# A graph layer and a routed expert layer on one core: slot heads one slot ahead, and results added by scatters into DRAM

## The chip, the cores and the metric

The kernel runs on one core of one Trainium2 chip. The metric is the device time of one execution in microseconds (us), the median of several. The other cores of the chip do nothing here.

## What is computed

There are 2048 nodes with 256 float32 features each. A first layer normalises every row, gathers neighbours along 67,584 weighted edges and adds the sums (and a per-node value) to the input. A second layer normalises again and sends every row to the best 2 of 8 experts. Cut to what matters:

```python
x = x + segment_sum(edge_weight[:, None] * layernorm(x)[dst], src) + node_vec1   # "x1" below
t = layernorm(x)
probs = softmax(t @ Wr + br)                      # 2048 x 8
top_p, top_idx = top_k(probs, 2)
weights = top_p / top_p.sum(-1, keepdims=True)
xn = layernorm(t)
# for each of the two experts e of a row:
h = gelu((xn * ln_g[e] + ln_b[e]) @ W1[e] + b1[e])          # 256 -> 1024
y = h @ W2[e] + b2[e]                                        # 1024 -> 256
out = x + weights[0] * y[top_idx[0]] + weights[1] * y[top_idx[1]]
```

So every output row is x1 plus two expert results, each multiplied by its weight.

## The kernel before

The first part (up to about 319 us of the profile) builds x1 in an SBUF tile `acc` of 128 partitions x 16 blocks x 256 and is the same in both kernels. Then a routing part ranks every (row, expert) pair and makes a dispatch list: the rows of each expert lie together, and each expert's rows are padded up to whole *slots* of 256 rows. There are at most 23 slots; 16 always exist, the others stand under conditions. Rows travel to their places in a DRAM buffer `xe_d` by 32 indirect DMAs (scatters) of 128 rows from the GpSimd queue. A row takes along its two expert numbers, its two weights and its token number (columns 256 to 260).

```python
y_d = dram.tile([2 * N + NS * TS, D], F32, name="y_d")       # N = 2048, NS = 23, TS = 256, D = 256
# ... routing ...
sent = []
for b in range(NB):                                          # NB = 16
    for i in range(2):
        st = nc.gpsimd.indirect_dma_start(out=xe_d[:, :],
            out_offset=bass.IndirectOffsetOnAxis(ap=rows_i[:, i, b:b + 1], axis=0),
            in_=xrow[:, b, :], in_offset=None)
        sent.append(st.ins.name)
# ... the bias b2, weighted, is added to acc by 16 small matmuls and adds (L556, L557) ...
```

Then the slots run one after the other. There are three sets of buffers; slot s + 2 is loaded while slot s computes. All loads go out on the SyncE queue, in this order per slot: the slot's rows, W1 of its expert (1 MB), a small tile of columns `ec` (bias and norm scales), W2 (1 MB).

```python
def load_slot(s):
    xs, w1, w2, ec = sets[s % len(sets)]
    ld = nc.sync.dma_start(xs, xe_v[s])                      # L592, waits for all 32 scatters of `sent`
    nc.sync.dma_start(w1, W1[e]...)                          # L595
    nc.sync.dma_start(ec, cols_d[e]...)                      # L596
    nc.sync.dma_start(w2, W2[e]...)                          # L597

def run_slot(s):
    # head: turn the rows (4 transposes of 128x128), scale them, find weight and target of each row
    for t in range(TT):                                      # TT = 2
        for k in range(KD):                                  # KD = 2
            nc.tensor.transpose(pt[:, k, ...], xs[:, t, ...], ident)       # L604, tile px
    for k in range(KD):
        nc.vector.tensor_scalar(xeT[:, k, :], pt[:, k, :], ec[...], ec[...], ...)   # L608
    # mine, wr, wt, any, to, to_i: eight small VectorE operations on 128x2 or 128x4 (L613 to L627);
    # to_i = 2 * token + (0 or 1), or a spare row for padding
    # body
    for c in range(KH):                                      # KH = 8
        ... ph = W1 chunk x xeT (2 matmuls, L633); hT[:, c] = gelu(ph) on ScalarE (L635)
    for t in range(TT):
        ... py = hT x W2 (8 matmuls, L639)
        nc.vector.tensor_scalar(ys, py, wt[:, t:t + 1], None, op0=OP.mult)          # L642
        nc.gpsimd.indirect_dma_start(out=y_d[:, :], out_offset=...to_i[:, t:t + 1]...,
                                     in_=ys, in_offset=None)                        # L643
```

Each float32 matmul of the code is recorded as two on the PE. At the end the two results of every row, which lie side by side in `y_d`, are read back (4 DMAs of 1 MB), added to `acc` by eight VectorE additions, and written out (4 DMAs of 512 KB):

```python
for q in range(NB // 4):
    ld = (nc.sync, nc.scalar)[q % 2].dma_start(yy, y_v[:, s, :])       # L672, waits for every scatter of results
    for r in range(2):
        nc.vector.tensor_add(acc[:, s, :], acc[:, s, :], yy[:, :, r * D:(r + 1) * D])   # L676
    (nc.sync, nc.scalar)[q % 2].dma_start(out_v[:, s, :], acc[:, s, :])  # L677
```

Of the kernel before, what the change touches and what calls it, by code (L numbers as in the profile page):

```python
# [20 lines left out]
P = 128  # L21
# [4 lines left out]
def kernel(  # L26
# [60 lines left out]
    for q in range(4):  # L87
# [32 lines left out]
    keep = consts.tile([P, NE, NB], F32, name="keep")  # L120
    nc.vector.memset(keep, 1.0)
    nc.vector.memset(keep[:, :, 0:1], 0.0)
    tok2 = consts.tile([P, NB], F32, name="tok2")
    nc.gpsimd.iota(tok2, pattern=[[2 * P, NB]], base=0, channel_multiplier=2,
                   allow_small_or_imprecise_dtypes=True)
    spare_r = consts.tile([P, NS, TT], F32, name="spare_r")
    nc.gpsimd.iota(spare_r, pattern=[[TS, NS], [P, TT]], base=2 * N, channel_multiplier=1,
                   allow_small_or_imprecise_dtypes=True)
    slot_e = consts.tile([P, NS], F32, name="slot_e")
    slot_i = consts.tile([1, NS + 1], I32, name="slot_i")  # L130
    xe_d = dram.tile([NS * TS, RW], F32, name="xe_d")
    y_d = dram.tile([2 * N + NS * TS, D], F32, name="y_d")
    cols_d = dram.tile([NE, P, KH + 2 * KD], F32, name="cols_d")
    none = consts.tile([P, RW], F32, name="none")
    nc.vector.memset(none, 0.0)
# [282 lines left out]

    with tc.tile_pool(name="route", bufs=1) as route, tc.tile_pool(
        name="xtT", bufs=3
    ) as xtTp, tc.tile_pool(name="ps_tr", bufs=3, space=PSUM) as ps_tr, tc.tile_pool(
# [1 line left out]
    ) as ps_lg, tc.tile_pool(name="ps_b2", bufs=2, space=PSUM) as ps_b2:  # L426
        xt = route.tile([P, NB, D], F32, name="xt")
        xrow = route.tile([P, NB, RW], F32, name="xrow")
        nc.vector.tensor_copy(xrow[:, :, D + 4:D + 5], tok2[:, :, None])
        nc.vector.memset(xrow[:, :, D + 5:], 0.0)  # L430
        mv, rs = stats(acc, "mva")
        for b in range(NB):
            normed(xt[:, b, :], acc[:, b, :], mv, rs, b)
# [120 lines left out]
        for b in range(NB):  # L554
            pb = ps_b2.tile([P, D], F32, name="pb")
            nc.tensor.matmul(pb, wgtT[:, b, :], b2_sb, start=True, stop=True)  # L556
            nc.vector.tensor_add(acc[:, b, :], acc[:, b, :], pb)  # L557


    got = []  # L560
    with tc.tile_pool(name="wpool", bufs=1) as wpool, tc.tile_pool(
        name="slot", bufs=2
    ) as slotp, tc.tile_pool(
        name="ps_x", bufs=1, space=PSUM
    ) as ps_x, tc.tile_pool(name="ps_h", bufs=4, space=PSUM) as ps_h, tc.tile_pool(
        name="ps_y", bufs=2, space=PSUM
    ) as ps_y:
        _, offs = nc.values_load_multi_w_load_instructions(
            slot_i[0:1, :NS], engines=[mybir.EngineType.SP], min_val=0, max_val=NE - 1,
            skip_runtime_bounds_check_because="a count of at most NE - 1 ends",  # L570
        )
        _, (n_slots,) = nc.values_load_multi_w_load_instructions(
            slot_i[0:1, NS:NS + 1], min_val=N * 2 // TS, max_val=NS,
            skip_runtime_bounds_check_because="the sum of the experts' slots",
        )
        xe_v = xe_d.rearrange("(s t p) c -> s p t c", t=TT, p=P)

        sets = []
        for i in range(AHEAD + 1):
            sets.append((  # L580
                wpool.tile([P, TT, RW], F32, name=f"xs{i}"),
                wpool.tile([P, KD, H], F32, name=f"w1_{i}"),
                wpool.tile([P, KH, D], F32, name=f"w2_{i}"),
                wpool.tile([P, KH + 2 * KD], F32, name=f"ec{i}"),
            ))

        def load_slot(s):
            if s >= NS:
                return
            e = ds(offs[s], 1)  # L590
            xs, w1, w2, ec = sets[s % len(sets)]
            ld = nc.sync.dma_start(xs, xe_v[s])  # L592
            for name in sent:
                tc.add_manual_dep(ld.ins, name, WAITS, reason="reads what it wrote")
            nc.sync.dma_start(w1, W1[e].rearrange("o (k p) h -> p (o k) h", p=P))  # L595
            nc.sync.dma_start(ec, cols_d[e].rearrange("o p c -> p (o c)"))  # L596
            nc.sync.dma_start(w2, W2[e].rearrange("o (c p) d -> p (o c) d", p=P))  # L597

        def run_slot(s):
            xs, w1, w2, ec = sets[s % len(sets)]  # L600
            pt = ps_x.tile([P, KD, TS], F32, name="px")
            for t in range(TT):
                for k in range(KD):
                    nc.tensor.transpose(pt[:, k, t * P:(t + 1) * P],  # L604
                                        xs[:, t, k * P:(k + 1) * P], ident)
            xeT = slotp.tile([P, KD, TS], F32, name="xeT")
            for k in range(KD):
                nc.vector.tensor_scalar(xeT[:, k, :], pt[:, k, :], ec[:, KH + k:KH + k + 1],  # L608
                                        ec[:, KH + KD + k:KH + KD + k + 1],
                                        op0=OP.mult, op1=OP.add)  # L610

            mine = slotp.tile([P, TT, 2], F32, name="mine")
            nc.vector.tensor_scalar(mine, xs[:, :, D:D + 2], slot_e[:, s:s + 1], None,  # L613
                                    op0=OP.is_equal)
            wr = slotp.tile([P, TT, 2], F32, name="wr")
            nc.vector.tensor_mul(wr, mine, xs[:, :, D + 2:D + 4])
            wt = slotp.tile([P, TT], F32, name="wt")
            nc.vector.tensor_reduce(wt, wr, AX.X, OP.add)
            spare = spare_r[:, s, :]
            any_ = slotp.tile([P, TT], F32, name="any")  # L620
            nc.vector.tensor_reduce(any_, mine, AX.X, OP.add)
            to = slotp.tile([P, TT], F32, name="to")
            nc.vector.tensor_sub(to, xs[:, :, D + 4], spare)
            nc.vector.tensor_mul(to, to, any_)
            nc.vector.tensor_add(to, to, mine[:, :, 1])
            to_i = slotp.tile([P, TT], I32, name="to_i")
            nc.vector.tensor_add(to_i, to, spare)  # L627

            hT = slotp.tile([P, KH, TS], F32, name="hT")
            for c in range(KH):  # L630
                ph = ps_h.tile([P, TS], F32, name="ph")
                for k in range(KD):
                    nc.tensor.matmul(ph, w1[:, k, c * P:(c + 1) * P], xeT[:, k, :],  # L633
                                     start=(k == 0), stop=(k == KD - 1))
                nc.scalar.activation(hT[:, c, :], ph, AF.Gelu, bias=ec[:, c:c + 1], scale=1.0)  # L635
            for t in range(TT):
                py = ps_y.tile([P, D], F32, name="py")
                for c in range(KH):
                    nc.tensor.matmul(py, hT[:, c, t * P:(t + 1) * P], w2[:, c, :],  # L639
                                     start=(c == 0), stop=(c == KH - 1))  # L640
                ys = slotp.tile([P, D], F32, name="ys")
                nc.vector.tensor_scalar(ys, py, wt[:, t:t + 1], None, op0=OP.mult)  # L642
                st = nc.gpsimd.indirect_dma_start(  # L643
                    out=y_d[:, :],
                    out_offset=bass.IndirectOffsetOnAxis(ap=to_i[:, t:t + 1], axis=0),
                    in_=ys,
                    in_offset=None,
                )
                tc.declare_no_dep(st.ins, group="got", reason="rows are unique")
                tc.add_to_no_dep_group("got", st.ins)  # L650
                got.append(st.ins.name)

        SURE = N * 2 // TS
        for s in range(AHEAD):
            load_slot(s)
        for s in range(SURE):
            load_slot(s + AHEAD)
            run_slot(s)
        with ExitStack() as nest:
            for s in range(SURE, NS):  # L660
                nest.enter_context(tc.If(n_slots > s))
                load_slot(s + AHEAD)
                run_slot(s)


    with tc.tile_pool(name="fin", bufs=4) as fin:
        out_v = out.rearrange("(b p) d -> p b d", p=P)
        y_v = y_d[:2 * N, :].rearrange("(b p r) d -> p b (r d)", p=P, r=2)
        for q in range(NB // 4):
            s = slice(4 * q, 4 * q + 4)  # L670
            yy = fin.tile([P, 4, 2 * D], F32, name="yy")
            ld = (nc.sync, nc.scalar)[q % 2].dma_start(yy, y_v[:, s, :])  # L672
            for name in got:
                tc.add_manual_dep(ld.ins, name, WAITS, reason="reads what it wrote")
            for r in range(2):
                nc.vector.tensor_add(acc[:, s, :], acc[:, s, :], yy[:, :, r * D:(r + 1) * D])  # L676
            (nc.sync, nc.scalar)[q % 2].dma_start(out_v[:, s, :], acc[:, s, :])  # L677


# [22 lines left out]
```

## Time and profile before

| | |
|---|---|
| time, median of 3 runs | 718.31 us (717.87 to 719.97) |
| span of the profiled execution | 719.2 us, mean granted TensorE clock 0.910 |
| PE busy, weight loads (PEld) busy | 538.0 us (75%), 468.5 us (65%) |
| VectorE, ScalarE, GpSimd busy | 314.8, 161.2, 99.6 us |
| DMA | 75.85 MB, mean 105 GB/s |

The execution falls into three parts: the graph layer up to 319 us, routing and dispatch from there to 414 us, and 18 slots (16 certain ones and two of the conditional ones) followed by the final sums. In the profile's groups, the two columns behind the bar are the busy time of a group and the mean duration of one instruction in ns, and then the idle time of the engine before them with the name of what ended it. PE is the matmul, PEld the weight load beside it, DVE VectorE, ACT ScalarE, POOL GpSimd; an engine with a q (SPq) is its queue of DMA issues. A DMA issue shows only when it was handed over; when it landed is read from who waited for it.

### The profile page before, as it was taken

Reading aid. Unit: us, or ns where it says so; the run is one execution under the profiler, and the core shown is the slowest. Engines: PE = TensorE matmul, PEld = TensorE weight load, DVE = VectorE, ACT = ScalarE, POOL = GpSimd, SP = SyncE. Lnnn points to the kernel's source line nnn. Section 1 sums busy time; section 2 is a strip of 40 time slices with the busy share of each in tenths; the row PEclk is TensorE's granted clock in tenths of the full one; section 3 lists DMA queues with packets and bytes.
Section 4 is the critical chain, followed back from the end, with each engine's and each line's share of the span. In section 5 each row is a group of like instructions: output and inputs, shape, how many; then the busy total and the mean of one; then the engine's idle time right before and its main releaser. Section 6 shows DMA issues by size and latency. Waiting matters only on the chain.

```text
span 719.2 us, 12356 instructions
## 1 busy us (share of the span) xinstructions
PE 538.0 (75%) x5244; PEld 468.5 (65%) x5244; DVE 314.8 (44%) x768; ACT 161.2 (22%) x309; POOL 99.6 (14%) x112
## 2 busy tenths in 40 slices
PE   0002789998998999968480099999999999999930
PEld 0001687897897889757340078888878888787730
DVE  6636999858947863137650022121121211211105
ACT  1001443135216205102100022222223222222200
POOL 1771000000000000000067301111111111111110
PEclk9999989999999999995555589999999999999985
DMA  8920000000000000000022495546456455565428
GB/s 258 349 53 19 2 3 3 1 3 3 2 1 3 3 1 3 2 0 1 0 77 108 147 375 195 193 148 198 162 168 198 156 175 181 156 197 176 132 69 298
DMA packets 53325, 75.85 MB, mean 105 GB/s; under 512 B 7320, under 2 KB 43024, under 8 KB 53264
## 3 DMA queue, kind: packets, MB, share of 16 engines
q1 hardware_dynamic: 44992, 58.00, 25.1%
q0 software_dynamic: 4672, 12.79, 5.0%
q10 hardware_dynamic: 3600, 4.22, 1.7%
q8 instruction: 43, 0.70, 0.4%
q14 instruction: 18, 0.15, 0.1%
HBM read 57.58 MB, written 17.41 MB: 104 GB/s over the span
## 4 chain that ended last, share of the span: by engine, by line
issue 27%; DMA 8%; POOL 8%; PE 7%; DVE 4%; SPq 0%; DVEq 0%; POOLq 0%; ACT 0%
DMA y_d<-ys,to_i 6%; POOL xe_d L524 4%; POOL y_d L643 4%; PE ph L633 2%; DMA yy<-y_d 2%; PE lg L443 2%; PE py L639 1%; PE pt L439 1%; DVE xrow L250 1%; DVE bn L241 1%; DMA ec<-cols_d 1%; DVE acc L676 0%; DMA xe_d<-xrow,rows_i 0%; DVE mva L242 0%; SPq L592 0%
## 5 line engine op out<-in xcount | busy, mean ns | idle before, releaser
L633 PE MATMUL ph<-xeT,w 128*128 128x256 f32 x576 | 131.1, 386 | 18.1 <-DVE xeT L608 18.1
L633 PEld LDWEIGHTS ph<-xeT,w 128*128 128x128 f32 x576 | 109.2, 192 | 37.2 <-DVE xeT L608 22.8
L639 PE MATMUL py<-w,hT 128*128 128x256 f32 x576 | 127.3, 379 | 0.0
L639 PEld LDWEIGHTS py<-w,hT 128*128 128x128 f32 x576 | 109.4, 190 | 14.9
L343 PE MATMUL py<-xn_sb,ac 128*128 128x256 f32 x512 | 118.1, 385 | 0.0
L635 ACT ACTIVATE hT<-ph,ec 128x256 f32<-128x256 f32 x144 | 66.6, 473 | 198.4 <-PE ph L633 198.4
L343 PEld LDWEIGHTS py<-xn_sb,ac 128*128 128x128 f32 x512 | 95.5, 193 | 12.5
L321 PE MATMUL pa<-hr,hl 128*128 128x32 bf16 x3072 | 89.2, 179 | 6.6 <-DVE hr L316 6.6
L321 PEld LDWEIGHTS <-hl 128*128 128x128 bf16 x3072 | 87.1, 98 | 9.3 <-issue 6.5
L642 DVE TENSOR_SCALAR ys<-py,wt 128x256 f32<-128x256 f32 x36 | 17.4, 484 | 143.9 <-PE py L639 143.9
L309 DVE TENSOR_TENSOR hl<-k,iota_b 128x4096 bf16<-128x4096 bf16 x32 | 73.1, 2285 | 5.6 <-ACT k L291 5.4
L524 POOL DMA_INDIRECT xe_d<-xrow,rows_i x32 | 31.1, 971 | 314.3 <-DVE acc L557 304.8
L643 POOL DMA_INDIRECT y_d<-ys,to_i x36 | 34.9, 970 | 253.4 <-DVE ys L642 211.1
L316 DVE TENSOR_TENSOR hr<-eq,w 128x1024 bf16<-128x1024 bf16 x96 | 60.4, 684 | 12.1 <-PE pa L321 12.1
L334 ACT COPY ac<-pt 128x512 f32<-128x512 f32 x64 | 37.7, 588 | 92.7 <-PE pt L333 92.7
L333 PE MATMUL pt<-ident,ar 128*128 128x128 f32 x256 | 44.9, 297 | 11.0 <-ACT ac L334 9.7
L323 ACT COPY ar<-pa 128x1024 f32<-128x1024 f32 x32 | 32.4, 1014 | 54.1 <-PE pa L321 54.1
L288 PE MATMUL pk<-ident,f 128*128 128x128 f32 x24 | 5.5, 321 | 51.7 <-DVE b_i L278 48.6
L333 PEld LDWEIGHTS pt<-ident,ar 128*128 128x128 f32 x256 | 28.8, 146 | 20.3 <-ACT ac L334 16.2
L345 DVE TENSOR_TENSOR acc<-acc,py 128x512 f32<-128x512 f32 x32 | 21.9, 684 | 41.9 <-PE py L343 41.9
L288 PEld LDWEIGHTS pk<-ident,f 128*128 128x128 f32 x24 | 3.0, 155 | 52.8 <-issue 48.9
L627 DVE TENSOR_TENSOR to_i<-to,spare_r 128x2 int32<-128x2 f32 x18 | 2.9, 161 | 78.6 <-DMA y_d<-ys,to_i 78.5
(146 smaller groups left out, 338.3 us busy)
## 6 DMA issues: line engine op xcount, KB each, us to landing
w<-in_L_ffn_W SPq DMA_DIRECT2D x40, 1024.0 KB
xe_d<-none SPq DMA_DIRECT2D x1, 6072.0 KB
xs<-xe_d SPq DMA_DIRECT2D x20, 264.0 KB, 6.2
yy<-y_d SPq DMA_DIRECT2D x2, 1024.0 KB
yy<-y_d ACTq DMA_DIRECT2D x2, 1024.0 KB
acc<-in_x ACTq DMA_DIRECT2D x2, 512.0 KB
acc<-in_x SPq DMA_DIRECT2D x2, 512.0 KB, 6.0
out<-acc SPq DMA_DIRECT2D x2, 512.0 KB, 3.5
```

The lines of the kernel that those rows point to most:

```text
L309: nc.vector.tensor_tensor(hl.rearrange("p g (n t) -> p g n t", t=2), two(k2[:, 0], g, P), pair(P), OP.is_equal)
L316: nc.vector.tensor_tensor(hr[:, i].rearrange("p g (n t) -> p g n t", t=2), eq_v, two(w2[:, i], g, RK), OP.mult)
L321: nc.tensor.matmul(pa[:, j, :], hl[:, j, :], hr[:, i, j, :], start=(i == 0), stop=(i == 2))
L323: nc.scalar.copy(ar_v[:, :, h * GH:(h + 1) * GH, :], pa.rearrange("p g (b c) -> p b g c", c=GC))
L333: nc.tensor.transpose(pt[:, i, :], ar[:, b + i, :], ident)
L334: nc.scalar.copy(ac[:, b:b + 4, :], pt)
L343: nc.tensor.matmul(pa[:, i, :], ac[:, b + i, :], xn_sb[:, cb + c, :], start=(c == 0), stop=(c == len(acs) - 1))
L524: st = nc.gpsimd.indirect_dma_start(out=xe_d[:, :], out_offset=bass.IndirectOffsetOnAxis(ap=rows_i[:, i, b:b + 1], axis=0), in_=xrow[:, b, :],
L633: nc.tensor.matmul(ph, w1[:, k, c * P:(c + 1) * P], xeT[:, k, :], start=(k == 0), stop=(k == KD - 1))
L635: nc.scalar.activation(hT[:, c, :], ph, AF.Gelu, bias=ec[:, c:c + 1], scale=1.0)
L639: nc.tensor.matmul(py, hT[:, c, t * P:(t + 1) * P], w2[:, c, :], start=(c == 0), stop=(c == KH - 1))
L643: st = nc.gpsimd.indirect_dma_start(out=y_d[:, :], out_offset=bass.IndirectOffsetOnAxis(ap=to_i[:, t:t + 1], axis=0), in_=ys, in_offset=None,)
```

## The change

Three things are changed, all in the routed part.

1. *Heads one slot ahead.* The head of slot s + 1 (transposes, scaling, targets) is put between the two matmul groups of slot s, so that its result is there when slot s + 1 begins. The tiles that pass from head to body (`xeT`, `wt`, `to_i`) become two fixed sets.
2. *Sums in DRAM.* `y_d` becomes one row per token, first filled with x1 (with its bias term) from `acc` by four DMAs on the ScalarE queue, and each slot's scatter adds its rows to it (`compute_op=OP.add`). A token is in two slots, so each slot's scatters wait for those of the slot before; the two of one slot do not wait for each other. Padding rows add zeros into 256 spare rows. At the end `y_d` is copied to the output, DRAM to DRAM, with no arithmetic. One small VectorE operation per slot goes away.
3. *Weights ahead of rows.* In `load_slot` W1 and `ec` are asked for before the rows. It is meant to let weights travel while the rows are still being scattered.

```diff
-    y_d = dram.tile([2 * N + NS * TS, D], F32, name="y_d")
+    y_d = dram.tile([N + TS, D], F32, name="y_d")
...
+            if b % 4 == 3:                       # after the bias was added to acc
+                nc.scalar.dma_start(
+                    y_d[:N, :].rearrange("(b p) d -> p b d", p=P)[:, b - 3:b + 1, :],
+                    acc[:, b - 3:b + 1, :])
...
         def load_slot(s):
+            nc.sync.dma_start(w1, W1[e].rearrange("o (k p) h -> p (o k) h", p=P))
+            nc.sync.dma_start(ec, cols_d[e].rearrange("o p c -> p (o c)"))
+            if s == 0:
+                load_rows(s, xs)
+            nc.sync.dma_start(w2, W2[e].rearrange("o (c p) d -> p (o c) d", p=P))
+            if s:
+                load_rows(s, xs)
+        def load_rows(s, xs):
             ld = nc.sync.dma_start(xs, xe_v[s])
             for name in sent:
                 tc.add_manual_dep(ld.ins, name, WAITS, reason="reads what it wrote")
-            nc.sync.dma_start(w1, ...); nc.sync.dma_start(ec, ...); nc.sync.dma_start(w2, ...)
...
         def run_slot(s):
...                                             # first matmul group and gelu
+            head(s + 1)
             for t in range(TT):
...
                     in_=ys,
                     in_offset=None,
+                    compute_op=OP.add,
                 )
-                tc.declare_no_dep(st.ins, group="got", reason="rows are unique")
+                tc.declare_no_dep(st.ins, group=f"slot{s}", reason="rows are unique in a slot")
...
+        head(0)
         for s in range(SURE):
             load_slot(s + AHEAD)
             run_slot(s)
...
-    (read back yy, eight additions onto acc, write out)
+    for q in range(4):
+        s = slice(q * N // 4, (q + 1) * N // 4)
+        (nc.sync, nc.scalar)[q % 2].dma_start(out[s, :], y_d[s, :])
```

More of the change, by code (lines that the diff above doesn't have):

```diff
@@ L122 @@
     nc.vector.memset(keep[:, :, 0:1], 0.0)
-    tok2 = consts.tile([P, NB], F32, name="tok2")
-    nc.gpsimd.iota(tok2, pattern=[[2 * P, NB]], base=0, channel_multiplier=2,
+    tok = consts.tile([P, NB], F32, name="tok")
+    nc.gpsimd.iota(tok, pattern=[[P, NB]], base=0, channel_multiplier=1,
                    allow_small_or_imprecise_dtypes=True)
-    spare_r = consts.tile([P, NS, TT], F32, name="spare_r")
-    nc.gpsimd.iota(spare_r, pattern=[[TS, NS], [P, TT]], base=2 * N, channel_multiplier=1,
+    spare_r = consts.tile([P, TT], F32, name="spare_r")
+    nc.gpsimd.iota(spare_r, pattern=[[P, TT]], base=N, channel_multiplier=1,
                    allow_small_or_imprecise_dtypes=True)
@@ L428 @@
         xrow = route.tile([P, NB, RW], F32, name="xrow")
-        nc.vector.tensor_copy(xrow[:, :, D + 4:D + 5], tok2[:, :, None])
+        nc.vector.tensor_copy(xrow[:, :, D + 4:D + 5], tok[:, :, None])
         nc.vector.memset(xrow[:, :, D + 5:], 0.0)
+        nc.sync.dma_start(y_d[N:, :].rearrange("(t p) d -> p t d", p=P),
+                          none[:, None, :D].to_broadcast([P, TT, D]))
         mv, rs = stats(acc, "mva")
@@ L557 @@
             nc.vector.tensor_add(acc[:, b, :], acc[:, b, :], pb)
-    got = []
+            if b % 4 == 3:
+                nc.scalar.dma_start(
+                    y_d[:N, :].rearrange("(b p) d -> p b d", p=P)[:, b - 3:b + 1, :],
+                    acc[:, b - 3:b + 1, :])
     with tc.tile_pool(name="wpool", bufs=1) as wpool, tc.tile_pool(
         name="slot", bufs=2
[L563 to L567, printed above, removed]
+    ) as slotp, tc.tile_pool(name="ps_x", bufs=1, space=PSUM) as ps_x, tc.tile_pool(
+        name="ps_h", bufs=4, space=PSUM
+    ) as ps_h, tc.tile_pool(name="ps_y", bufs=2, space=PSUM) as ps_y:
         _, offs = nc.values_load_multi_w_load_instructions(
@@ L585 @@
             ))
+        heads = []
+        for i in range(2):
+            heads.append((
+                wpool.tile([P, KD, TS], F32, name=f"xeT{i}"),
+                wpool.tile([P, TT], F32, name=f"wt{i}"),
+                wpool.tile([P, TT], I32, name=f"to_i{i}"),
+            ))
         def load_slot(s):
@@ L594, in load_slot, with head @@
                 tc.add_manual_dep(ld.ins, name, WAITS, reason="reads what it wrote")
[L595 to L599, printed above, removed]
+        def head(s):
+            if s >= NS:
+                return
             xs, w1, w2, ec = sets[s % len(sets)]
+            xeT, wt, to_i = heads[s % 2]
             pt = ps_x.tile([P, KD, TS], F32, name="px")
@@ L605, in run_slot @@
                                         xs[:, t, k * P:(k + 1) * P], ident)
-            xeT = slotp.tile([P, KD, TS], F32, name="xeT")
             for k in range(KD):
@@ L616, in run_slot @@
             nc.vector.tensor_mul(wr, mine, xs[:, :, D + 2:D + 4])
-            wt = slotp.tile([P, TT], F32, name="wt")
             nc.vector.tensor_reduce(wt, wr, AX.X, OP.add)
-            spare = spare_r[:, s, :]
             any_ = slotp.tile([P, TT], F32, name="any")
@@ L622, in run_slot @@
             to = slotp.tile([P, TT], F32, name="to")
-            nc.vector.tensor_sub(to, xs[:, :, D + 4], spare)
+            nc.vector.tensor_sub(to, xs[:, :, D + 4], spare_r)
             nc.vector.tensor_mul(to, to, any_)
-            nc.vector.tensor_add(to, to, mine[:, :, 1])
-            to_i = slotp.tile([P, TT], I32, name="to_i")
-            nc.vector.tensor_add(to_i, to, spare)
+            nc.vector.tensor_add(to_i, to, spare_r)
+        def run_slot(s):
+            xs, w1, w2, ec = sets[s % len(sets)]
+            xeT, wt, to_i = heads[s % 2]
             hT = slotp.tile([P, KH, TS], F32, name="hT")
@@ L647, in run_slot @@
                     in_offset=None,
+                    compute_op=OP.add,
                 )
-                tc.declare_no_dep(st.ins, group="got", reason="rows are unique")
-                tc.add_to_no_dep_group("got", st.ins)
-                got.append(st.ins.name)
+                tc.declare_no_dep(st.ins, group=f"slot{s}", reason="rows are unique in a slot")
+                tc.add_to_no_dep_group(f"slot{s}", st.ins)
         SURE = N * 2 // TS
@@ L663 @@
                 run_slot(s)
[L666 to L677, printed above, removed]
+    for q in range(4):
+        s = slice(q * N // 4, (q + 1) * N // 4)
+        (nc.sync, nc.scalar)[q % 2].dma_start(out[s, :], y_d[s, :])
 _INS = ["x", "src", "dst", "edge_weight", "node_vec1", "L0_ffn_Wr", "L0_ffn_br", "L0_ffn_ln_g",
```

## The prediction

> **What bounds the kernel now.** I read the page's slices first, then the chain that ended last, then the instructions in order of time, because the change touches only the part after 362 us.
>
> ```profile
> PE   0002789998998999968480099999999999999930
> DMA  8920000000000000000022495546456455565428
> ```
>
> Each digit is a slice of 18 us. In the slots (slices 23 to 38) PE is at 9 and the DMA engines at about half: the slots are bound by PE, and transfers have room. At both ends of the slots PE is idle: slices 20 to 22 (dispatch) and 38 to 39 (final sums). What lies between PE's work in a slot is seen in time order, first for certain slots, then for the two conditional ones:
>
> ```profile
> 445.50 0.60 PE L604 MATMUL px<-ident,xs 128*128 128x128 f32 x4
> 446.14 1.00 DVE L608 TENSOR_SCALAR xeT<-px,ec 128x256 f32<-128x256 f32 x2
> 446.47 0.97 POOL L643 DMA_INDIRECT y_d<-ys,to_i  x1 [2.48 <-DVE ys L642]
> 446.75 7.17 PE L633 MATMUL ph<-xeT,w 128*128 128x256 f32 x32 [0.64 <-DVE xeT L608]
> 452.73 0.16 DVE L627 TENSOR_TENSOR to_i<-to,spare_r 128x2 int32<-128x2 f32 x1 [5.52 <-DMA y_d<-ys,to_i]
> ...
> 660.03 7.20 PE L633 MATMUL ph<-xeT,w 128*128 128x256 f32 x32 [1.73 <-DVE xeT L608]
> ...
> 676.16 7.19 PE L633 MATMUL ph<-xeT,w 128*128 128x256 f32 x32 [1.60 <-DVE xeT L608]
> ```
>
> The brackets are idle time of the engine and what ended it. After the transposes (px) PE waits 0.64 us for VectorE to copy them out (xeT); in a conditional slot VectorE does the small target operations first, and PE waits 1.73 and 1.60 us. A slot in a table of windows, one certain and one conditional:
>
> ```profile
> 446.75:461.90 15.15, 14.51 (x68) 12.57 (x69) 2.86 (x13) 3.70 (x8) 1.93 (x3) 1.00 0.53 174
> 659.96:676.10 16.14, 14.54 (x68) 12.49 (x68) 2.81 (x14) 3.79 (x8) 1.94 (x2) 1.00 0.51 162
> ```
>
> The first number is the period, the second PE's busy time; the rest are the other engines, clock, DMA share and GB/s. So 14.5 us is the floor of a slot with this arithmetic, and 0.64 or 1.6 us per slot can be had. The other gap in PE's work is the tail:
>
> ```profile
> 691.07 0.97 POOL L643 DMA_INDIRECT y_d<-ys,to_i  x1 [2.48 <-DVEq L659]
> 696.55 0.92 SPq L672 DMA_DIRECT2D yy<-y_d  x2
> 704.45 1.23 DVE L676 TENSOR_TENSOR acc<-acc,yy 128x1024 f32<-128x1024 f32 x1 [13.66 <-DMA yy<-y_d]
> 708.32 5.25 SPq L677 DMA_DIRECT2D out<-acc  x2
> 709.67 4.63 DVE L676 TENSOR_TENSOR acc<-acc,yy 128x1024 f32<-128x1024 f32 x4 [0.24 <-DMA yy<-y_d]
> ```
>
> From the last scatter to the end of the span (719.2) are 28.1 us: 4.9 until it has landed (the chain has SyncE go on at 695.95), 0.6 to the first read, about 13 for 4 MB of reads, the last additions to 714.3, and 4.9 for the last writes. The start of slot 0:
>
> ```profile
> 408.28 1.09 PE L604 MATMUL px<-ident,xs 128*128 128x128 f32 x4 [33.49 <-DMA xs<-xe_d]
> 408.27 0.39 SPq L595 DMA_DIRECT2D w<-in_L_ffn_W  x1
> 413.92 1.00 DVE L608 TENSOR_SCALAR xeT<-px,ec 128x256 f32<-128x256 f32 x2 [4.57 <-DMA ec<-cols_d]
> ```
>
> The rows are there at 408.3, but `ec`, queued behind W1, lands at 413.8, and the first slot begins at 414.5.
>
> **What the Trainium skill says.** On the page DMA: Bandwidth & Descriptors, four places. "Rules for kernel authors": an accumulating DMA reads its destination and writes it later and nothing holds the bytes in between, so an earlier DMA's semaphore must be awaited. That is why slots are now chained; no run before has such a DMA. "Two DMAs through the same engine are not ordered": two read-modify-write packets of one row collided when adjacent, and not with five or more packets between; I take from it that an engine overlaps several such packets instead of finishing each. "Anatomy of one DMA": some 2 us of fixed cost per DMA, most of it the receipt of the last write. The trace's unloaded scatter takes 4.9 us from the start of POOL's instruction, of which 0.97 is POOL, so more than that page's figure. "Latency and other measured facts": copies between DRAM tensors ran at about 207 to 214 GB/s per direction when the layout was kind. This trace has no such copy.
>
> **The change, part by part.**
>
> *Heads ahead.* The built program's order on PE is now first group, 4 transposes, second group, and the copy-out has the 7 us of the second group to finish. I keep the 0.60 us of transposes and take away the waits. 15 transitions between slots 0 to 15 by 0.64 us are 9.6 us; the two into slots 16 and 17 give 1.73 + 1.60 = 3.3 us. Slot 17 now makes a head for a slot 18 that does not run: 0.6 us lost. Sum −12.3 us.
>
> *Weights ahead.* The built program settles it: the first W1 load waits for all eight lanes of scatters at the same counts as the rows did before, because its buffer lies where the routing part's tiles lay and those are released together. So nothing travels during the 40 us of scatters. The order only turns round: W1, `ec`, rows, W2. Before, W1's issue to `ec` landed took 413.8 − 408.3 = 5.5 us. Now W1 should be issued at about 405.8, since the rows' issue and the register loads are out of its way. `ec` is then there at about 411.3, the rows (264 KB at some 380 GB/s, 0.7 us) at 412.0, transposes 1.1 and copy-out 0.6 make 413.7 against 414.5. I book −0.5 us.
>
> *Filling y_d.* Four 512 KB writes on ScalarE's queue, released by the bias additions at about 366 to 375 us. In that stretch the scatters leave the DMA engines mostly free, and the first accumulating scatter is 50 us away. 0 us.
>
> *Accumulating scatters.* Call L the time from the start of a scatter's instruction on POOL to its landing. Before, it is 452.73 − 446.47 = 6.3 us under load. Now each row is also read first: an estimate of 2 us more, from half of the unloaded 3.9 us that lie behind POOL's 0.97. So L is 8 to 9 us. Who waits for it? POOL: the first scatter of a slot comes about 11 us after the last of the slot before (14.5 − 3.5). VectorE: in the built order it stands at `to_i` of slot s + 2 until slot s's scatters have landed, then has xeT (1.0) and the first ys of slot s + 1 to do, which is due 7.2 + 0.6 + 3.5 = 11.3 us after the last ys. With L near 9 both are met and the sum is 0; above about 11 us every extra us goes into all slots.
>
> *Tail.* Last landing 4.9 + 2 = 6.9 us after its issue; 0.6 to the first copy and 0.9 for two issues per queue. Then 2 MB DRAM to DRAM. The trace's reads ran at about 385 GB/s and its final writes at about 350, that is 5.4 and 6.0 us if each had the memory alone. Fully overlapped that is 6, one after the other 11.4; the skill's 207 to 214 GB/s gives 10. I take 8.7, plus 2 us for start and receipt and 0.5 to the end: 19.6 against 28.1, −8.5 us.
>
> Sum: −12.3 − 0.5 − 8.5 = −21.3, so 718.3 − 21.3 = 697.0 us.
>
> **The rivals.** *The chain of scatters becomes the bound.* If accumulation is slow (rows handled one after the other, or starved beside the weight loads), the period becomes L + 3: landing, then xeT, ys, and two instructions on POOL. L = 13 makes a slot 16 us, about +1.5 x 17 = 25 us over the wished 14.5: some 722. L = 16 gives about 770. For it: VectorE already stands 78.5 us in all at `to_i` for plain scatters. Against it: DMA share 0.53, and only 128 rows, 8 per engine, in each. *The copy at the end is slow.* Its shape is 16 pieces of 32 KB, one per engine; at half the assumed rate it takes 17 instead of 9 us, and the tail gains nothing: 705. *PE is not freed:* the second group must now begin after the transposes, or slot 1's rows, now queued behind its 2 MB of weights, come late for a head that is asked for 7 us earlier. By bytes: 4.5 MB at 375 GB/s from 405.8 is 417.8, and the head is due at about 422.5. A miss would cost 1 to 3 us once.
>
> **Range and chances.** Small errors: tail ±4, heads ±2, start ±2. The tail to the slow side is the accumulating scatter. I give that rival about one chance in five of costing anything, and one in ten of costing more than the heads save. Middle 697, range 686 to 716. Faster by over 2% means below 703.9: 0.72. Within 2%: 0.16. Slower, above 732.7: 0.12.
>
> **What would show it.** Right: ph of slots 1 to 17 with no wait for xeT; a period of 14.4 to 14.6 us in both kinds of slot; the first W1 load issued only after the last scatter into `xe_d`; some 19 to 20 us from last scatter to end. Wrong: POOL or `to_i` waiting on y_d until the next slot's ys is due, PE waiting for ys or for free py buffers, a period above 15; or copies of more than 12 us. The prediction fails if accumulation lands later than about 11 us, and less so if the final copy is slow.

## The result and the profile after

| | before | after |
|---|---|---|
| median time, us | 718.63 (717.87 to 719.97) | 688.52 (687.74 to 691.02) |
| ratio to before, 95% interval | | 0.9585 (0.9555 to 0.9615) |
| profiled span, us | 719.2 | 687.4 |
| PE busy | 538.0 us (75%) | 533.0 us (78%) |
| GpSimd busy | 99.6 us | 120.5 us |

The kernel is 30.1 us faster, where 21.3 were predicted. The slices of the page of after (40 slices of 17.2 us; the slots begin with the sixteenth digit from the right; PEclk is the granted TensorE clock in tenths):

```profile
PE   0001778999999899994936009999999999999990
PEclk9999999999999999998555558999999999999996
```

PE stands at 9 through all the slots and drops only at the two ends. The clock line shows something that the old page had as well and that matters below: in the idle slices ahead of the slots the granted clock is at 5.

**The slots.** A table of windows from the first matmul of slot 0 to the first of slot 17, for after (columns: stretch, its length, then busy time and instructions of PE, PEld, VectorE, ScalarE and GpSimd, granted clock, DMA share, GB/s), with the window of a single conditional slot (16) below it:

```profile
411.83:656.65 244.82, 244.82 (x1156) 215.19 (x1157) 51.66 (x187) 65.70 (x137) 51.37 (x33) 0.99 0.68 198
...
642.40:656.65 14.25, 14.25 (x69) 12.55 (x68) 2.82 (x11) 3.80 (x8) 3.11 (x2) 1.00 0.64 185
```

The same 17 slots in the same table of before:

```profile
414.52:676.16 261.64, 248.73 (x1156) 215.11 (x1156) 48.83 (x205) 64.14 (x137) 32.97 (x34) 0.99 0.58 188
```

They took 261.64 and take 244.82 us: 16.8 less. PE was idle for 261.64 − 248.73 = 12.9 us and is idle for none. But the busy time of the same 1156 matmuls fell as well, by 3.9 us, at the same mean clock. So part of what the page counted as busy went with the stops. Where it sat is seen in time order in slot 16 of after:

```profile
642.40 7.07 PE L650 MATMUL ph<-xeT,w 128*128 128x256 f32 x32
643.37 1.55 POOL L661 DMA_INDIRECT y_d<-ys,to_i  x1 [1.90 <-DVE mine L631]
649.31 0.60 PE L624 MATMUL px<-ident,xs 128*128 128x128 f32 x4
649.71 0.16 DVE L641 TENSOR_TENSOR to_i<-to,spare_r 128x2 int32<-128x2 f32 x1 [5.89 <-DMA y_d<-ys,to_i]
649.75 7.07 PE L657 MATMUL py<-w,hT 128*128 128x256 f32 x32
649.95 0.99 DVE L627 TENSOR_SCALAR xeT<-px,ec 128x256 f32<-128x256 f32 x2
654.16 1.55 POOL L661 DMA_INDIRECT y_d<-ys,to_i  x1 [9.25 <-DVE ys L660]
656.65 7.07 PE L650 MATMUL ph<-xeT,w 128*128 128x256 f32 x32
```

The first group is recorded as 7.07 us long, yet the transposes begin 6.91 us after its start; they are recorded as 0.60, yet the second group begins 0.44 after them. The ends overlap what follows by 0.16 us. A slot is 6.91 + 0.44 + 6.90 = 14.25 us, in certain and conditional slots alike. Before, the transposes to the next group took 1.25 us (0.60 and the wait of 0.64 shown in the prediction), because PE had to stop there, and the first group behind the stop is recorded 0.10 us longer (7.17, in the prediction, against 7.07). So a stop cost 0.64 us of idle time (more in a conditional slot) and 0.26 of busy time: 0.16 of lost overlap and 0.10 in the next group. 17 times 0.26 are 4.4 us, of which slot 0's longer first group (9.60 us against 9.09) takes 0.5 back.

The Trainium skill, page Perfetto Trace Analysis, section "Tensor Engine Instruction (MATMUL, LD_WEIGHTS)", says that the end time of a TensorE instruction is estimated, not observed. Whether that is behind the overlap of 0.16 us is not shown. VectorE begins to copy the transposes out 0.64 us after their start (649.95), right behind their recorded end, so a group may really end beside the start of the next. The starts of the groups do not depend on it.

The bracket at the second line is a scatter issued right after its ys, the one at `to_i` is VectorE waiting until it landed: 649.71 − 643.37 = 6.3 us after its start (over the 17 slots 4.2 to 7.7, median 6.0). The next ys comes at 653.40, when PE has its py ready; VectorE had stood idle 2.46 us for it. So nobody is late, but a landing some 2.5 us later would have delayed that ys; in other slots VectorE's idle time there is 0.6 to 2.5 us. Two groups of the page tell the same for all slots:

```profile
L661 POOL DMA_INDIRECT y_d<-ys,to_i x36 | 56.0, 1556 | 215.5 <-DVE ys L660 155.9
...
L641 DVE TENSOR_TENSOR to_i<-to,spare_r 128x2 int32<-128x2 f32 x19 | 3.1, 161 | 97.1 <-DMA y_d<-ys,to_i 97.0
```

VectorE idles 97.1 us at `to_i`, which costs nothing, and an accumulating scatter keeps GpSimd for 1.556 us where the plain one took 0.97.

**The start of slot 0** in time order, from the last dispatch scatter:

```profile
400.92 0.97 POOL L525 DMA_INDIRECT xe_d<-xrow,rows_i  x1 [0.30 <-DMA xe_d<-xrow,rows_i]
...
405.89 0.72 SPq L601 DMA_DIRECT2D w<-in_L_ffn_W  x1
407.11 0.43 SPq L610 DMA_DIRECT2D xs<-xe_d  x1
410.10 1.09 PE L624 MATMUL px<-ident,xs 128*128 128x128 f32 x4 [37.11 <-DMA xs<-xe_d]
411.83 9.60 PE L650 MATMUL ph<-xeT,w 128*128 128x256 f32 x32 [0.64 <-DVE xeT L627]
```

W1 is asked for only after the last scatter, so nothing travels ahead. From the last scatter to slot 0 are 10.9 us, where before had 414.52 − 402.75 = 11.8. Slot 1's rows, which the prediction feared would come late behind the weights, are there at 419.5, and its transposes begin at 422.6.

**The tail** in time order, then the source view of the line that closes the program, with its queue instructions (duration in ns: least, median, greatest; then first and last start):

```profile
671.87 1.55 POOL L661 DMA_INDIRECT y_d<-ys,to_i  x1 [1.90 <-DVEq L679]
677.50 1.22 SPq L688 DMA_DIRECT2D out<-y_d  x2
677.51 1.48 ACTq L688 DMA_DIRECT2D out<-y_d  x2
```

```profile
L709 POOLq DRAIN  x3: 51/107/4837, 677.6 to 687.1; - x3
```

The copy is issued 5.6 us after the start of the last scatter and the span ends 9.9 us later: 15.5 us for the tail instead of 28.1. Beside the copy GpSimd runs a drain of 4.8 us; it will matter in an experiment. The windows of the tail show bytes of the copy from 678.5 to 684.0, with the DMA engines busy and 393 GB/s in the middle (last column):

```profile
680.00:684.00 4.00, 0.00 (x0) 0.00 (x0) 0.00 (x0) 0.00 (x0) 0.00 (x0) 0.50 1.11 393
```

So of the 9.9 us about 1 passes before the first bytes, 5.5 with them and 3.4 from the last bytes to the end.

The bookkeeping of the two profiles: start of dispatch −1.8 (it comes out of the untouched part; the last dispatch scatter starts anywhere from 398.9 to 402.8 us in the kernels here), dispatch itself 39.5 us in both, start of slot 0 −0.9, slots −16.8, last slot's body with its surplus head +0.3, tail −12.6: together −31.8, the difference of the spans.

### The profile page after: what moved, and what is told of

It reads as the page before. It is cut to its first block, busy times and chain, and to the rows that moved or that the text cites. A ratio compares the mean times of both kernels' runs of the same rounds, so it can differ in the third digit from the quotient of the medians.

```text
span 687.4 us, 12332 instructions
## 1 busy us (share of the span) xinstructions
PE 533.0 (78%) x5248; PEld 467.6 (68%) x5248; DVE 309.8 (45%) x751; ACT 162.9 (24%) x309; POOL 120.5 (18%) x112
## 5 line engine op out<-in xcount | busy, mean ns | idle before, releaser
L650 PEld LDWEIGHTS ph<-xeT,w 128*128 128x128 f32 x576 | 111.1, 193 | 16.6 <-DVE xeT L627 1.0
L657 PEld LDWEIGHTS py<-w,hT 128*128 128x128 f32 x576 | 108.0, 190 | 13.9
L652 ACT ACTIVATE hT<-ph,ec 128x256 f32<-128x256 f32 x144 | 68.2, 474 | 180.8 <-PE ph L650 180.4
L661 POOL DMA_INDIRECT y_d<-ys,to_i x36 | 56.0, 1556 | 215.5 <-DVE ys L660 155.9
L316 DVE TENSOR_TENSOR hr<-eq,w 128x1024 bf16<-128x1024 bf16 x96 | 60.4, 682 | 12.1 <-PE pa L321 12.1
L641 DVE TENSOR_TENSOR to_i<-to,spare_r 128x2 int32<-128x2 f32 x19 | 3.1, 161 | 97.1 <-DMA y_d<-ys,to_i 97.0
L624 PE MATMUL px<-ident,xs 128*128 128x128 f32 x76 | 11.9, 281 | 37.1 <-DMA xs<-xe_d 37.1
```

The source lines that it names most:

```text
L316: nc.vector.tensor_tensor(hr[:, i].rearrange("p g (n t) -> p g n t", t=2), eq_v, two(w2[:, i], g, RK), OP.mult)
L661: st = nc.gpsimd.indirect_dma_start(out=y_d[:, :], out_offset=bass.IndirectOffsetOnAxis(ap=to_i[:, t:t + 1], axis=0), in_=ys, in_offset=No ...
```

## The experiments

Four questions: does each part bring what the bookkeeping says, are the accumulating scatters near to binding, is the order of loads worth anything, and what is left at both ends? The time of before beside each batch was 718.2 to 719.5 us; all ratios are to it.

**Heads alone.** Before, with only the head moved (its three tiles in two fixed sets).

```diff
+            head(s + 1)              # between the two groups of run_slot(s)
             for t in range(TT):
                 py = ps_y.tile([P, D], F32, name="py")
...
+        head(0)
```

> The kernel before with the heads one slot ahead and nothing else: plain scatters, rows first, old final sums. Theory A (the transposes share PE's pipeline, so a slot falls to the 14.25 us seen after the change): 17 transitions save 16.8 us, the surplus head of slot 18 costs 0.3, so about 702 us. Theory B (the sum of the prediction: only the recorded waits vanish, 12.3 us): about 706 us, period 14.5.

702.6 us, ratio 0.9764 (0.9739 to 0.9789). Time order:

```profile
657.44 7.07 PE L644 MATMUL ph<-xeT,w 128*128 128x256 f32 x32
```

No bracket at ph: PE does not wait, and the period is again 14.25 us. The tail, from the last scatter's start at 672.65 to 701.0, is 28.4 us, about as before. So the heads alone are worth 16.9 us, as theory A said, and need nothing of the other parts.

**All but the heads.** After, with the head back at the beginning of its own slot.

```diff
         def run_slot(s):
+            head(s)
...
-            head(s + 1)
...
-        head(0)
```

> The changed kernel with each head back at the start of its own slot: accumulating scatters, final copy and weights first stay. Theory A: 16.5 us slower than the changed kernel, about 705 us, periods of 15.1 us or slightly less (one small VectorE operation fewer), and the tail stays near 15.5 us. Theory B (the heads gave only 12.3 us and something else, unnamed, the rest): about 701 us.

706.63 us, ratio 0.9818 (0.9795 to 0.9841). The wait is back, as this line of the time order shows:

```profile
673.61 7.19 PE L651 MATMUL ph<-xeT,w 128*128 128x256 f32 x32 [1.40 <-DVE xeT L627]
```

The tail is 16.0 us. What is left without the heads is 12.9 us, close to the tail's 12.6, and the two parts add: 16.9 + 12.9 = 29.8 of 30.1. In the profiles the 17 slots take 261.7 us here and 244.5 with the heads alone.

**Rows first.** After, with the rows asked for ahead of W1.

```diff
         def load_slot(s):
+            load_rows(s, xs)
             nc.sync.dma_start(w1, ...)
             nc.sync.dma_start(ec, ...)
-            if s == 0:
-                load_rows(s, xs)
             nc.sync.dma_start(w2, ...)
-            if s:
-                load_rows(s, xs)
```

> The changed kernel with rows, W1, ec, W2 asked for in the old order. Theory A (no weight travels during the scatters, only the order behind the wait turns round): 0.5 to 1.5 us slower than the changed kernel, 689 to 690 us. Rival (weights ahead of rows is worth what it is meant to bring, some 1 MB of transfer): 3 us slower or more.

689.49 us, ratio 0.9583 (0.9561 to 0.9606). The times alone do not separate it from after; the time order does:

```profile
413.24 8.86 PE L647 MATMUL ph<-xeT,w 128*128 128x256 f32 x32 [5.37 <-DVE xeT L624]
```

The transposes are early and PE then waits 5.37 us for a copy-out that needs `ec`. Slot 0 begins 12.2 us after the last dispatch scatter instead of 10.9. The order is worth about 1.3 us at this point, and nothing in the other slots. Part of it is lost again in slot 0, whose first group is 8.86 us long here and 9.60 in after: slot 1 begins 28.2 against 27.7 us after the last dispatch scatter.

**Plain scatters.** After without the addition: rows overwrite each other, so the sum is left out.

```diff
                     in_offset=None,
-                    compute_op=OP.add,
                 )
```

> The changed kernel with the addition taken out of the scatters (compute_op left away, all waits kept). It leaves out the sum of x1 and the two results: a row keeps what was written last. Theory A (the accumulation is hidden, and costs 0.6 us of GpSimd per scatter): same time within 1 us, GpSimd 0.97 instead of 1.55 us per scatter, latency from start to landing 0.5 to 1 us shorter. Rival (the accumulating scatters hold slots back, or stretch the tail by the 2 us that the prediction gave them): 2 us faster or more.

686.98 us, ratio 0.9545 (0.9525 to 0.9566): 1.5 us less than after, between the two expectations, with intervals that still touch. Time order:

```profile
656.76 0.97 POOL L661 DMA_INDIRECT y_d<-ys,to_i  x1 [2.48 <-DVE to L639]
662.88 0.16 DVE L641 TENSOR_TENSOR to_i<-to,spare_r 128x2 int32<-128x2 f32 x1 [5.80 <-DMA y_d<-ys,to_i]
```

A plain scatter lands 6.1 us after its start here (5.9 in the slot before) against 6.8 and 6.3 with the addition; the medians of the 17 slots are 5.4 and 6.0. GpSimd's instruction is 0.58 us shorter, which is about all of that difference. At the tail the copy is issued 5.0 instead of 5.6 us after the scatter. The slots' period is 14.25 us either way. The tail is 0.6 of the 1.4 us between the two profiles; the rest lies at the start of slot 0 and in its first group, and differs as much between other kernels in which these places are alike (slot 0 begins 10.2 to 10.9 us after the last dispatch scatter).

**Both scatters of a slot in one chain.** After without the declaration that they are independent, so each waits for the landing of the one before.

```diff
-                tc.declare_no_dep(st.ins, group=f"slot{s}", reason="rows are unique in a slot")
-                tc.add_to_no_dep_group(f"slot{s}", st.ins)
```

> The changed kernel with the two scatters of a slot chained as well, each waiting for the one before. This doubles the latency in the chain of slots. With L = 6.8 us from a scatter's start to its landing, the loop is two landings, then VectorE's to_i, xeT (1.0) and ys (0.5), then 0.3 to the next scatter: 2 x 6.8 + 2.1 = 15.7 us per slot. Theory A (the loop through POOL and VectorE is the slack that the prediction worked out): period about 15.7 us, 1.4 x 17 = 25 us slower, about 713 us. Rival (buffers absorb it, only POOL waits): within 5 us of the changed kernel.

689.2 us, ratio 0.959 (0.9572 to 0.9609): no change, where 713 was expected. Time order of one slot:

```profile
609.30 1.57 POOL L661 DMA_INDIRECT y_d<-ys,to_i  x1 [8.45 <-DVE ys L660]
613.83 1.56 POOL L661 DMA_INDIRECT y_d<-ys,to_i  x1 [2.96 <-DMA y_d<-ys,to_i]
618.30 0.16 DVE L641 TENSOR_TENSOR to_i<-to,spare_r 128x2 int32<-128x2 f32 x1 [5.82 <-DMA y_d<-ys,to_i]
```

The two links take 4.53 and 4.47 us, not the 6.8 that I had taken from after's last slot. Chaining hardly lengthens the stretch from a slot's first start to its last landing: it is 8.5 to 10.1 us over the slots, and 8.7 to 10.7 in after, where PE sets the two starts 3.45 us apart. Two links and the way from landing to the next scatter (2.1 us, measured in the experiment of four links below) make about 11.1 us, below the period of 14.25. Is there such a loop at all, then?

**Four links.** The same chain, with a second accumulating scatter of zeros to the same rows after each.

```diff
                     compute_op=OP.add,
                 )
+                nc.gpsimd.indirect_dma_start(
+                    out=y_d[:, :],
+                    out_offset=bass.IndirectOffsetOnAxis(ap=to_i[:, t:t + 1], axis=0),
+                    in_=none[:, :D], in_offset=None, compute_op=OP.add)
-                tc.declare_no_dep(...)
-                tc.add_to_no_dep_group(...)
```

> The changed kernel with every scatter followed by one that adds a tile of zeros to the same rows, all four of a slot chained one behind the other. It adds zeros and leaves nothing out. Chained scatters were seen to take 4.0 to 5.4 us from start to the next start, so the loop is four of these and then 2.1 us of VectorE and waits: 4 x 4.5 + 2.1 = 20.1 us against PE's 14.25. Theory A (the loop through POOL and VectorE is real, and two links of 4.5 us had left it 3 us short of PE): period about 20 us, 5.8 x 17 = some 100 us slower than the changed kernel, about 790 us. Rival (no such loop: POOL can fall behind without holding PE): within 15 us of the changed kernel.

843.59 us, ratio 1.1739 (1.1719 to 1.1758), where about 790 was expected. Time order of a slot:

```profile
614.81 9.36 PE L650 MATMUL ph<-xeT,w 128*128 128x256 f32 x32 [7.16 <-DVE xeT L627]
615.88 1.55 POOL L661 DMA_INDIRECT y_d<-ys,to_i  x1 [6.00 <-DVE mine L631]
619.93 1.55 POOL L668 DMA_INDIRECT y_d<-none,to_i  x1 [2.50 <-DMA y_d<-ys,to_i]
624.45 1.55 POOL L661 DMA_INDIRECT y_d<-ys,to_i  x1 [2.97 <-DMA y_d<-none,to_i]
630.99 1.55 POOL L668 DMA_INDIRECT y_d<-none,to_i  x1 [4.99 <-DMA y_d<-ys,to_i]
637.88 0.16 DVE L641 TENSOR_TENSOR to_i<-to,spare_r 128x2 int32<-128x2 f32 x1 [21.17 <-DMA y_d<-none,to_i]
638.95 9.23 PE L650 MATMUL ph<-xeT,w 128*128 128x256 f32 x32 [7.43 <-DVE xeT L627]
```

The loop is real. Four links of 4.05, 4.52, 6.54 and 6.89 us and 2.14 from the landing to the next slot's first scatter make 24.14, which is the period (638.95 − 614.81). PE waits over 7 us in slots 2 to 14 for xeT, which on VectorE stands behind `to_i`. So the first rival of the prediction is shown as a mechanism. The sum gives it a threshold: the chain binds when the stretch from a slot's first scatter to its last landing exceeds 14.25 − 2.1 = 12.1 us. The threshold itself was not tested, only points on both sides (9.0 in the slot of the chain of two, 22.0 here). The same stretch in after, where nothing ties the two scatters of a slot together, is 8.7 to 10.7 us. It includes the 3.45 us between the two starts, which could shrink, so how much slower a landing could be in after before it costs time was not tested.

The expected time was too low because two of the four links are longer than 4.5 us. In this slot the links differ by up to 2.8 us. From 798 us on, when the weight loads have ended (40 GB/s or less in all), one start follows the other after 4.0 to 4.6 us; that loads are what slows the others is likely, but was not tested by itself.

**Weights in memory of their own.** After, with the weight buffers allocated before the routing tiles, not in their place.

```diff
     gnn.close()
+    wpool = ctx.enter_context(tc.tile_pool(name="wpool", bufs=1))
...
-    with tc.tile_pool(name="wpool", bufs=1) as wpool, tc.tile_pool(
+    with tc.tile_pool(
         name="slot", bufs=2
```

> The changed kernel with the weight buffers taken from their own memory, not from that of the routing tiles, so the first W1, W2 and ec can load while rows are scattered. Theory A (the shared memory was what held the weights): first W1 issued at about 364 us instead of 406, first slot begins when its rows have landed, about 408.5 instead of 411.8, so 3 us faster than the changed kernel, about 685.5 us. Rival (weights are not what the first slot waits for, or they slow the scatters): within 1 us of the changed kernel, or slower.

685.0 us, ratio 0.953 (0.9505 to 0.9555). Time order:

```profile
365.92 0.41 SPq L602 DMA_DIRECT2D w<-in_L_ffn_W  x1
...
400.65 0.97 POOL L526 DMA_INDIRECT xe_d<-xrow,rows_i  x1 [0.30 <-DMA xe_d<-xrow,rows_i]
403.10 0.37 SPq L611 DMA_DIRECT2D xs<-xe_d  x1
...
407.80 8.99 PE L651 MATMUL ph<-xeT,w 128*128 128x256 f32 x32 [0.64 <-DVE xeT L628]
```

The first W1 is asked for at 365.92, and now only the rows wait for the scatters; slot 0 begins 7.2 us after the last one, not 10.9. This is what the third part of the change was meant to do. With the new order of issues it was the shared memory that held the weights back. Whether the new order is needed beside it was not tested.

**Sums straight into the output.** After, with x1 written to the output, the scatters adding there, and padding rows dropped by a bound instead of going to spare rows. No final copy.

```diff
-    y_d = dram.tile([N + TS, D], F32, name="y_d")
...
-                    out=y_d[:, :],
+                    out=out[:, :],
...
+                    bounds_check=N - 1,
+                    oob_is_err=False,
                     compute_op=OP.add,
...
-    for q in range(4):
-        ...dma_start(out[s, :], y_d[s, :])
```

> The changed kernel with x1 written into the output itself and the scatters adding there; padding rows get a row number beyond the end and are skipped, the final copy is gone. Theory A (the copy's 9.9 us from issue to end lie wholly on the path): 9 to 10 us faster, about 679 us. Rival (padding rows, now skipped, or the end of the program cost as much, or the output is slower to add to): within 3 us of the changed kernel.

684.4 us, ratio 0.9515 (0.9484 to 0.9545): 4.1 us less than after, where 9 to 10 were expected. The time order has its last scatter here, and the source view of the closing line follows:

```profile
670.92 1.55 POOL L658 DMA_INDIRECT out<-ys,to_i  x1 [1.90 <-DVEq L678]
```

```profile
L705 POOLq DRAIN  x3: 51/107/4837, 676.6 to 682.0; - x3
```

The copy is gone, yet 11.4 us remain from the last scatter to the end at 682.3. GpSimd's drain of 4837 ns, from 676.6 to 681.4, is now the last long piece. In after the same 4837 ns lay beside the copy. So the copy's visible part was 4.1 us, the rest of it was in parallel with something that stays.

**Both of these together.**

```diff
+    wpool = ctx.enter_context(tc.tile_pool(name="wpool", bufs=1))
...
-                    out=y_d[:, :],
+                    out=out[:, :],
...
+                    bounds_check=N - 1,
+                    oob_is_err=False,
...
-        (nc.sync, nc.scalar)[q % 2].dma_start(out[s, :], y_d[s, :])
```

> Both of the last two together: weight buffers in their own memory, and sums in the output itself. The two gains lie in different places, so they should add: about 12 to 13 us faster than the changed kernel, about 676 us. If one of them only moves a wait to the place of the other, less.

679.85 us, ratio 0.9452 (0.9429 to 0.9475), the fastest version of the study. The gains add within the spread of the runs: 3.5 and 4.1 apart, 8.7 together, and slot 0 begins 7.1 us after the last dispatch scatter. The expected 676 still had the 9 to 10 us of the copy in it.

**And the Gelu table loaded early.** The last version, with a one-column Gelu after the writes of x1, so that its table is in place. The question was whether the first group (9.80 us in the last version, 7.07 in other slots) is slow by the table load or by the clock.

```diff
+        warm = consts.tile([P, 1], F32, name="warm")
+        nc.scalar.activation(warm, acc[:, NB - 1, 0:1], AF.Gelu, bias=0.0, scale=1.0)
```

> Weights in their own memory and sums in the output itself, and one gelu of a single column on ScalarE during the dispatch, so that its table is loaded by then. In the changed kernel the first slot's first matmul group took 9.6 us against 7.07 in the others, with a table load of 1.28 us in it. Theory: the group falls to about 7.1 us, 2 to 2.5 us faster than the version without the early table, about 677.5 us. Rival (the first group is slow because TensorE comes from idle with a lower clock): no change, about 680 us.

681.2 us, ratio 0.948 (0.9464 to 0.9496). Time order, then the table of windows for the tile ph alone (columns after the length: busy time of PE, PEld and ScalarE, clock, DMA share, GB/s):

```profile
374.96 1.28 ACT L562 ACT_TABLE_LOAD   x1 [13.75 <-DMA ec<-cols_d]
...
409.19 9.86 PE L650 MATMUL ph<-xeT,w 128*128 128x256 f32 x32 [0.64 <-DVE xeT L627]
```

```profile
409.00:413.00 4.00, 3.81 (x9) 3.09 (x10) 0.47 (x1) 0.50 1.04 384
413.00:417.00 4.00, 4.00 (x16) 3.36 (x16) 1.90 (x4) 0.79 1.06 343
417.00:421.00 4.00, 2.05 (x10) 1.47 (x8) 1.42 (x3) 1.00 0.24 41
```

The table was loaded 34 us ahead and the first group is no shorter. It is the clock: 9 matmuls in the first 4 us at 0.50, 16 in the next at 0.79, then 1.00. A rival is left, the loads beside it (DMA share 1.04). The kernel with four links, whose groups after a stop of 7.2 us take 9.36 us, settles it:

```profile
614.81:618.81 4.00, 4.00 (x9) 3.21 (x10) 1.80 (x7) 0.65 (x2) 1.55 (x1) 0.50 0.22 23
618.81:622.81 4.00, 4.00 (x19) 3.49 (x18) 0.00 (x0) 2.04 (x5) 1.55 (x1) 0.94 0.27 30
```

(Busy time of all five engines here, then clock, DMA share, GB/s.) Again 9 matmuls in 4 us at 0.50, with hardly any transfers and no table load.

The Trainium skill, page TensorE: Matmul & The Clock Gate, section "What's actually happening", says that an idle PE is clocked at half and comes to full speed after at least one busy window of about 3.4 us. The trace agrees in kind. From 0.79 in the second window the half clock lasted until about 414.7 (4 us of which 1.7 at 0.50), that is 5.5 us after the group's start; worked out in the same way it was 3.4 us in the kernel with the rows first (0.50 to 416 us, 0.66 from 416 to 417).

## Why the prediction was right

697.0 was predicted, 688.5 measured, inside the range of 686 to 716 but near its lower end, with the right sign and in the main the right mechanism. By its steps:

- *Heads ahead, −12.3: mechanism right, size too small.* Measured −16.8 and +0.3, alone 16.9 (heads alone) and 17.2 (30.1 less the 12.9 of all but the heads). The mis-sized term is the floor of a slot. I read PE's busy time of 14.51 as work and called it the floor; without a stop a slot is 14.25, below the 14.4 to 14.6 that were to show the prediction right. PE's idle time of 12.9 us was right, but the stops also cost 3.9 us that the table counted as busy: the transposes take 0.44 us of PE, not 0.60, and the group behind a stop is 0.10 longer. The surplus head cost 0.3, not 0.6 us.
- *Weights ahead, −0.5: the wait right, the size partly luck.* The first W1 did wait for the scatters. That it was issued at 405.89, with 405.8 predicted, is chance: the dispatch ended 1.8 us earlier. Counted from the last scatter, W1 came after 5.0 us and not 3.1, and from W1 to slot 0 passed 5.9 us and not 7.9, since the rows landed 4.2 us after W1's issue, not 6.2. The two errors cancel: 10.95 us from the last scatter to slot 0 were predicted, 10.91 measured.
- *Filling y_d, 0: right so far as seen.* Dispatch takes 39.5 us in both kernels.
- *Accumulating scatters, hidden: right, with L too high.* 8 to 9 us were estimated, 4.2 to 7.7 measured, median 6.0. The 2 us for reading each row first are not there: with the addition a scatter lands about 0.5 us later after its start, about what GpSimd's longer instruction makes. The rival's loop exists, as four links show. The prediction's limit of 11 us is for one landing and the 12.1 us are for the whole stretch of a slot's scatters, so they are not the same quantity. An L near 9, as estimated, would have used up VectorE's idle time before ys (in slot 16 6.3 + 2.5 = 8.8).
- *Tail, −8.5: mechanism right, size too small.* Measured −12.6. Until the copy's issue 5.6 instead of 7.5 (the 2 us of accumulation again); copy to the end 9.9 instead of 12.1, of which 0.9 was booked for the second issue of each queue. The mis-sized term here is the transfer, 5.5 us instead of 8.7. It ran at 393 GB/s over its middle 4 us, so above the 207 to 214 GB/s that the Trainium skill (page DMA: Bandwidth & Descriptors, section "Latency and other measured facts") gives for copies of another layout and that the prediction leaned on, and close to the 6 us that the prediction gave for reads and writes fully overlapped.
- *Not foreseen:* nothing that changed the verdict. The start of dispatch 1.8 us earlier is in untouched code and accounts for the rest of the difference between the two profiles.

## What to carry to other kernels

Where an engine has a short stop in every round, the gain of removing it can be larger than the idle time the table shows: compare the starts of successive groups, not their recorded durations. Before removing a piece at the end of a program or reordering loads at its start, ask what lies beside it or beneath it: the copy's removal uncovered GpSimd's drain, and the reordered loads still waited for the memory of the routing tiles. A new chain is judged by the sum of its links against the period: here a chain of 11.1 us cost nothing against 14.25, and one of 24.1 set the period.

## What the runs showed of the hardware

- An accumulating scatter of 128 rows of 1 KB costs GpSimd 1.556 us, a plain one 0.97, and lands hardly later: 6.0 us after its start (median of after's slots) against 5.4 (plain scatters).
- With four links chained, the scatters landed 4.0 to 6.9 us after their start in one and the same slot.
- GpSimd ends each program here with a drain that begins about when the last scatter has landed. It took 4.84 us in after and in the version without the copy, 8.23 in the three kernels with plain scatters (before, heads alone, plain scatters), where it runs beside the reads or the copy, and 3.52 with four links. What sets its length was not tested.
- After the idle dispatch PE runs the first 3.4 to 5.5 us of slot 0 at half clock, so the first group takes 8.9 to 9.9 us instead of 7.07. With four links a stop of 7.2 us was enough: PE's work ends at 607.7, and the granted clock is 1.00 from 611 to 612, 0.72 from 612 to 613 and 0.50 from 613 on. Stops of 0.64 to 1.73 us, in before, left it at 1.00.
